# Row maxima taken by segments with a later look, and the row's own share added on VectorE

## The chip, the core and the metric

The kernel runs on one core of one Trainium2 chip, in one launch. The time is the device time of an execution in microseconds (us). The core has five engines that the text calls PE (TensorE, matrix products), DVE (VectorE), ACT (ScalarE), POOL (GpSimd) and SP (SyncE, which here only issues transfers). Each engine takes its instructions in the order in which the built program has them, and waits at an instruction until what it needs is there. Transfers between the device memory and the on-chip memory are issued by SP, by ACT and, where rows are picked by a list of indices, by POOL. An instruction of the kernel is named by its line, L623 say, and by the tile it writes and the tiles it reads, `tops<-ar`.

## The reference

Four graph layers follow each other on the same 2708 nodes with 512 features each. Each normalises x, applies relu, and adds its result to x. `adj` is a 2708 by 2708 matrix, almost all zeros, with entries of 0.05 to 5.42 where it is not zero, more of them at low node numbers.

```python
# layer 0
head = (adj > 0).astype(float)
head = head / maximum(sqrt(sum(head * head, -1, keepdims=True)), 1e-12)
inc = adj + head
x = x + (inc @ h) / sum(inc, -1, keepdims=True)
# layer 1: attention with the mask  -1e16 * (1 - maximum(adj, eye))
atts = atts - 1e16 * (1.0 - adj_with_diag)
x = x + softmax(atts) @ values @ Wo
# layer 2: two graph convolutions and a projection
# layer 3: (adj != 0) @ (h @ W + b) / column counts
```

In layer 1 the term 1e16 * adj is so large that each row's softmax picks one node: the column of the largest entry of `maximum(adj, eye)`. So layer 1 needs, for each row, the largest entry, its column, and the second largest entry (the kernel has a general path for the case that the two are too close, which these data do not take).

## The kernel before, in words

The rows are cut into 22 tiles m of 128 rows (`NT` = 22; the last has 20). The first stage, `with tc.tile_pool(name="l0_slab", ...)` up to L920, does layer 0, the search for the row maxima of layer 1, and the lists of nonzero columns that all later stages use. It takes the first 460 us. The instructions are ordered by a scheduler that plans with its own estimates of durations; the order on each engine is then fixed in the built program.

What is done for a row tile is spread over several functions:

- `stats_to(m)` runs ahead of the products: it loads the tile's rows of `adj` (a slab of 128 by 2708, `load_slab`, L563), counts signs and sums on ACT (`row_norm`, `row_sum`), and then calls `attended`. The tiles of `LATE` (0 to 5) are loaded again at the end of the stage, and `attended` is called for them there (L890 to L895).
- `attended(m)` (L617) sets the diagonal of the slab to at least 1 (L622) and searches the 2708 columns: `max` gives the eight largest entries of each row (L623), `max_index` their columns (L624). Only the first two values and the first column are used: `flags` compares the two values (L281), and `idx` (L914) is the list by which layer 1 fetches rows.
- `search(m)` finds the nonzero columns of a group from running counts (`max_index`, L461) and writes the indices `idx_g` and `idx_a`.
- `gathers_to(m)` issues on POOL, per chunk of 128 listed columns, one gather of entries of `adj` (`ac`, L635, 64 KB) and one of rows of the normalised x (`h`, L654, 256 KB). The row buffers are the tiles h6 to h21, so a gather has to wait until PE is done with what the buffer held. `CHUNKS` has 8 to 5 chunks per tile for the tiles 3 to 20.
- `incidence(m)` makes the weights: `inc` for the first (dense) column tiles and `incl` for the listed ones (L698, L706 on DVE). For the tiles 6 to 20 (`alone`), the diagonal entry is treated apart: ACT makes `own`, the row's own normalised x times its weight (L727), and the product of `ident` and `own` is one more pair in the sum (L728).
- The main loop (L854) multiplies the pairs on PE into `acc` (L866), scales by 1 over the degree and adds x on DVE (`xt`, L879), normalises, and one or two tiles later `after` makes the projection (`yacc`, L176) and stores `y`.

For the tiles 1 and 2 the entries are gathered at the end of the stage (L903) and stored to `listed` by POOL itself (L645). The next stage begins with `fetch` (L1166): a gather on POOL of rows of `y` by `idx` (L1172), which needs `idx` and every store of `y`.

DVE waits for ACT, PE and loads, and PE waits for DVE's `inc`; POOL waits for `idx_a` and `idx_g` from DVE, for the row buffers from PE and for the chunk buffers `ac` (three of them) from the stores to `listed`.

Of the kernel before, what the change touches and what calls it, by code (L numbers as in the profile page):

```python
# [9 lines left out]
FP = mybir.dt.float32  # L10
# [3 lines left out]
U32 = mybir.dt.uint32  # L14
U8 = mybir.dt.uint8
I32 = mybir.dt.int32
AF = mybir.ActivationFunctionType
ALU = mybir.AluOpType
AX = mybir.AxisListType
# [3 lines left out]
P = 128  # L23
LN_EPS = 1e-5
NORM_EPS = 1e-12
MASK_SCALE = 1e16
# [18 lines left out]
def kernel(  # L45
# [27 lines left out]
    nc = tc.nc  # L73

    N, D = x.shape
    H, _, DK = wk_d.shape
    NT = (N + P - 1) // P
    NFULL = N // P
# [4 lines left out]
    UNIT = 4  # L83
# [81 lines left out]
    nc.gpsimd.memset(ones_b, 1.0)  # L165


    adj_units = bass.AP(adj_t.tensor, 0, [[UNIT, N * N // UNIT], [1, UNIT]])

    def span(t):  # L170
# [73 lines left out]
    with tc.tile_pool(name="l0_slab", bufs=2) as slabs, tc.tile_pool(  # L244
        name="l0_h", bufs=1
# [14 lines left out]

        idx_a = hp.tile([P, NT, NCH], U32, name="idx_a")

        tops = hp.tile([P, NT, 8], FP, name="tops")
        at_top = hp.tile([P, NT, 8], U32, name="at_top")
        cnts, sums_sgn, ends, caps = (
            hp.tile([P, NT], FP, name=name) for name in ("cnts", "sums_sgn", "ends", "caps")
        )
# [5 lines left out]
        if TAIL:  # L273
            nc.gpsimd.memset(tops[:, NFULL, :], 0.0)
            nc.gpsimd.memset(tops[:, NFULL, 0:1], 2.0)
            nc.gpsimd.memset(at_top[:, NFULL, :], 0)

        def flags():

            score = wp.tile([P, NT, 2], FP, name="score", bufs=1)  # L280
            nc.vector.tensor_scalar(  # L281
                score, tops[:, :, 0:2], 1.0, MASK_SCALE, op0=ALU.subtract, op1=ALU.mult
            )
            nc.vector.tensor_tensor(bad[:, :NT], score[:, :, 1], score[:, :, 0], ALU.is_ge)
            nc.vector.tensor_tensor(
                bad[:, BAD_NEG : BAD_NEG + NT], sums_sgn, cnts, ALU.not_equal
            )
            nc.vector.tensor_tensor(bad[:, BAD_MANY : BAD_MANY + NT], ends, caps, ALU.is_gt)
# [17 lines left out]
        nc.gpsimd.iota(place_i, pattern=[[P, NCH]], base=1, channel_multiplier=1)  # L306
        places = hp.tile([P, NCH], FP, name="places")
        nc.vector.tensor_copy(places, place_i)

        pending, pending_c = [], []  # L310

# [253 lines left out]
        def count_signs(m, last):  # L565

            sgn = slabs.tile([P, N], BF, name="sgn", bufs=GROUP)
            behind(sgn[:1, :1], last)
            nc.scalar.activation(sgn, slab[m], AF.Sign, accum_out=sums_sgn[:, m : m + 1])
            nc.scalar.activation(sgn, sgn, AF.Relu, accum_out=cnts[:, m : m + 1])  # L570
# [46 lines left out]
        def attended(m):  # L617

            n = rows(m)
            cols = slice(m * P, m * P + n)  # L620
            ar = slab.pop(m)
            nc.vector.tensor_max(ar[:n, cols], ar[:n, cols], ident[:n, :n])  # L622
            nc.vector.max(tops[:n, m, :], ar[:n])  # L623
            nc.vector.max_index(at_top[:n, m, :], tops[:n, m, :], ar[:n])  # L624

        gathers, gather_slot = {}, [0]

# [60 lines left out]
        def incidence(m):  # L688
# [31 lines left out]
            if alone(m):  # L720
                c = diag_c[:, m : m + 1]
                by = wp.tile([P, 3], FP, name="by")
                nc.scalar.activation(by[:, 2:3], c, AF.Sign)
                nc.scalar.activation(by[:, 2:3], by[:, 2:3], AF.Identity, scale=rn, bias=c)
                nc.scalar.activation(by[:, :2], kept[:, :, m], AF.Copy, scale=by[:, 2:3])
                own = wp.tile([P, D], FP, name="own", bufs=1)
                nc.scalar.activation(own, xs[m], AF.Relu, scale=by[:, 0:1], bias=by[:, 1:2])  # L727
                pairs.append((ident, own))  # L728
            if m >= LEAD:
                ac, gs = gathers.pop(m)  # L730
                pending.append(lambda: nc.sync.dma_start(out=listed[m], in_=ac))
# [30 lines left out]
        def stats_to(m):  # L762


            while normed[0] <= order_n.index(m):
                t = order_n[normed[0]]
                do_next()
                load_slab(t)
                if normed[0] + 1 < NT:
                    load_slab(order_n[normed[0] + 1])  # L770
                row_norm(t)
                row_sum(t)
                if t == 0 or t % GROUP == GROUP - 1 or t >= NT - 2:
                    last_block = count(masks)
                    if t not in ZERO:
                        if dense_of(t):
                            rank_blocks(list(masks), last_block)
                        else:
                            flush_counts()
                            todo.append(partial(rank_rows, list(masks)))  # L780
                        todo.extend(partial(search, k) for k in masks)
                        do_next(0)
                    masks.clear()
                if t in LATE:
                    slab.pop(t)
                else:
                    attended(t)
                normed[0] += 1
# [65 lines left out]
        for m in range(NT):  # L854
# [37 lines left out]
                load_slab(LATE[step])  # L892
            if 0 < step <= len(LATE):
                count_signs(LATE[step - 1], xt[:1, :1])
                attended(LATE[step - 1])  # L895
            if m + 8 == NT + 1:
                todo.append(partial(rank_rows, list(range(1, LEAD))))
                todo.extend(partial(search, k) for k in range(1, LEAD))
# [12 lines left out]
                )  # L911
                wr = load_w(wset, w3_d, "wr")
        flush()
        nc.vector.tensor_copy(idx, at_top[:, :, 0])  # L914
        degrees()
        after(NT - 2, None)
        after(NT - 1, hns.pop(NT - 1))
# [1035 lines left out]
```

## Time and profile before

| what | value |
|---|---|
| time, median of 14 runs | 1352.41 us (1347.33 to 1361.07) |
| the profiled execution | 1352.61 us, span 1350.2 us |
| PE busy | 1199.0 us (89%) |
| DVE busy | 924.1 us (68%) |
| ACT busy | 694.3 us (51%) |
| POOL busy | 676.4 us (50%) |
| SBUF and HBM transfers | 349.92 MB, mean 259 GB/s |
| L623 and L624, 22 instructions each | 65.3 us each, mean 2970 and 2968 ns |
| gathers of entries `ac` on POOL (L635), 130 | 136.3 us, mean 1049 ns |
| gathers of rows `h` on POOL (L654), 111 | 115.8 us, mean 1044 ns |

The shares are of the whole span, over stages with different limits; the first stage is about a third of it. A row of a timeline gives the start and the duration in us, the engine, the line, the operation, out<-in, the shapes, and in brackets how long the engine had been idle and what ended that ("issue": nothing that the profile shows). A row of groups gives the count, then busy us and mean ns of one, then the idle time just before them. A row of waits gives who waited for whom, the us in total, the times, and the longest.

### The profile page before, as it was taken

What the parts mean: (1) busy time and instruction counts of PE and PEld (TensorE: products, weight loads), DVE (VectorE), ACT (ScalarE), POOL (GpSimd) and SP (SyncE); (2) the same over time, 40 slices, a digit from 0 to 9 for tenths busy, and PEclk for the clock granted to TensorE, in tenths of its full rate; (3) what the DMA queues carried; (4) which work ended last, traced back from release to release, by engine and by line L of the source; (5) the groups of instructions that cost most, each with busy time, mean ns of one, the idle gap of its engine ahead of it and who ended that gap; (6) DMA issues with size and microseconds to landing.
All of it is one profiled execution on the core that took longest, in us unless ns stands there. A gap on an engine that the chain in (4) does not pass through costs nothing.

```text
span 1350.2 us, 15148 instructions
## 1 busy us (share of the span) xinstructions
PE 1199.0 (89%) x4223; PEld 714.9 (53%) x4223; DVE 924.1 (68%) x1859; ACT 694.3 (51%) x1098; POOL 676.4 (50%) x703
## 2 busy tenths in 40 slices
PE   4988989998869389989999989899999999978897
PEld 2333444444423166646665656466666766656665
DVE  3777989998999589643444456256777677666676
ACT  5886377687365456432232334145555554555463
POOL 2237467777883511055554542354444444167763
PEclk9998999999889689999999999899999999988999
DMA  9988989999895697378877886866665656488885
GB/s 344 340 303 280 324 306 326 366 328 342 288 349 206 201 308 256 105 241 259 270 243 262 287 268 214 260 214 206 196 200 191 208 185 208 151 310 295 287 283 157
DMA packets 179341, 349.92 MB, mean 259 GB/s; under 512 B 22794, under 2 KB 85524, under 8 KB 175516
## 3 DMA queue, kind: packets, MB, share of 16 engines
q1 hardware_dynamic: 131648, 201.72, 44.0%
q0 software_dynamic: 46032, 145.05, 33.0%
q10 hardware_dynamic: 1568, 2.10, 0.4%
q8 instruction: 35, 0.57, 0.2%
q14 instruction: 58, 0.48, 0.1%
HBM read 285.97 MB, written 62.82 MB: 258 GB/s over the span
## 4 chain that ended last, share of the span: by engine, by line
PE 51%; DMA 21%; DVE 15%; issue 6%; POOL 3%; ACT 3%; SPq 1%; DVEq 0%; ACTq 0%; POOLq 0%
PE aggs L1110 14%; PE main L1010 8%; PE agg L1106 6%; PE mixed L1010 4%; PE acc L866 4%; PE yacc L176 3%; PE aggs L1106 3%; PE pt L983 2%; DVE found L461 2%; POOL ac L635 2%; DMA wb<-hid 2%; DMA nz<-nz 2%; DVE tops L623 2%; DMA h<-h0d,idx_g 1%; DMA ac<-g1d 1%
## 5 line engine op out<-in xcount | busy, mean ns | idle before, releaser
L1047 POOL DMA_INDIRECT gg<-g2d,idx_g x130 | 143.3, 1102 | 194.6 <-PE aggs L1110 138.7
L1110 PE MATMUL aggs<-gg,ac 128*128 128x512 f32 (+1 forms) x520 | 231.5, 593 | 2.9 <-DMA gg<-g1d,idx_g 2.1
L1047 POOL DMA_INDIRECT gg<-g1d,idx_g x130 | 131.3, 1010 | 155.3 <-PE aggs L1110 85.2
L635 POOL DMA_INDIRECT ac<-in_adj_t_dram,idx_a x130 | 136.3, 1049 | 69.6 <-issue 31.8
L866 PE MATMUL acc<-h,inc 128*128 128x512 f32 (+1 forms) x276 | 134.6, 631 | 27.7 <-DVE inc L706 22.5
L1110 PEld LDWEIGHTS aggs<-gg,ac 128*128 128x128 f32 (+1 forms) x520 | 96.9, 188 | 113.7 <-issue 99.3
L654 POOL DMA_INDIRECT h<-h0d,idx_g x111 | 115.8, 1044 | 47.0 <-issue 19.8
L866 PE MATMUL acc<-h,incl 128*128 128x512 f32 (+1 forms) x222 | 103.7, 607 | 0.0
L866 PEld LDWEIGHTS acc<-h,inc 128*128 128x128 f32 (+1 forms) x276 | 52.2, 201 | 86.4 <-issue 51.4
L176 PE MATMUL yacc<-wvo,hT 128*128 128x512 f32 (+1 forms) x176 | 83.8, 615 | 1.4 <-ACT hT L211 1.4
L1075 DVE SCALAR_TENSOR_TENSOR ac<-ac,diag_c,bias 128x512 f32<-128x512 f32 x30 | 22.6, 752 | 88.1 <-DMA ac<-g1d 53.8
L1047 POOL DMA_INDIRECT gg<-hidr,idx_g x62 | 66.5, 1072 | 27.8 <-issue 13.9
L1106 PE MATMUL agg<-glo,a_lo 128*128 128x512 f32 x180 | 73.5, 408 | 4.6 <-ACT glo L225 4.6
L1106 PE MATMUL agg<-ghi,a_hi 128*128 128x512 f32 x180 | 77.3, 430 | 0.0
L1106 PE MATMUL aggs<-gs,a_s 128*128 128x512 f32 x180 | 73.5, 408 | 1.3 <-DVE gs L222 1.3
L990 DVE SCALAR_TENSOR_TENSOR v_lo<-pt,v_hi 128x512 fp32r<-128x512 f32 (+1 forms) x88 | 56.8, 656 | 16.1 <-ACT v_hi L989 15.8
L866 PEld LDWEIGHTS acc<-h,incl 128*128 128x128 f32 (+1 forms) x222 | 41.1, 191 | 48.4 <-issue 43.6
L1139 DVE SCALAR_TENSOR_TENSOR u<-aggs,u 128x512 f32<-128x512 f32 x42 | 28.8, 687 | 55.0 <-PE aggs L1110 54.8
L623 DVE MAX8 tops<-ar 128x8 f32<-128x2708 f32 (+1 forms) x22 | 65.3, 2970 | 0.0
L624 DVE FIND_INDEX8 at_top<-tops,ar 128x8 uint32<-128x2708 f32 (+1 forms) x22 | 65.3, 2968 | 0.0
L583 ACT ACTIVATE sgn<-ar 128x2708 bf16<-128x2708 f32 (+1 forms) x22 | 54.1, 2458 | 17.1 <-DMA ar<-in_adj_dram 17.1
L989 ACT ACTIVATE v_hi<-pt 128x512 fp32r<-128x512 f32 (+1 forms) x88 | 48.1, 575 | 24.9 <-PE pt L983 24.8
(355 smaller groups left out, 2758.8 us busy)
## 6 DMA issues: line engine op xcount, KB each, us to landing
ar<-in_adj_dram SPq DMA_DIRECT2D x27, 1354.0 KB
raw<-in_adj_t_dram SPq DMA_DIRECT2D x92, 192.0 KB
slot<-x SPq DMA_DIRECT2D x41, 256.0 KB
at<-in_adj_t_dram SPq DMA_DIRECT2D x26, 256.0 KB
h<-in_x_dram SPq DMA_DIRECT2D x21, 256.0 KB
h0d<-h POOLq DMA_DIRECT2D x21, 256.0 KB, 7.4
xt<-in_x_dram SPq DMA_DIRECT2D x21, 256.0 KB
x<-xt SPq DMA_DIRECT2D x21, 256.0 KB
```

Of the source, the lines that this page charges most:

```text
L176: nc.tensor.matmul(acc[:n], hT[:, c, :n], w[:, c, :], start=(c == 0), stop=(c == NCD - 1))
L583: nc.scalar.activation(sgn[:n], ar[:n], AF.Sign, accum_out=sum_sgn[:n])
L623: nc.vector.max(tops[:n, m, :], ar[:n])
L624: nc.vector.max_index(at_top[:n, m, :], tops[:n, m, :], ar[:n])
L635: nc.gpsimd.indirect_dma_start(out=ac[:, c, :n], out_offset=None, in_=adj_units, element_offset=dense_of(m) * P * N + m * P, in_offset=bas ...
L654: nc.gpsimd.indirect_dma_start(out=g, out_offset=None, in_=h0d[:, :], in_offset=bass.IndirectOffsetOnAxis(ap=index_g(m)[:, c : c + 1], axi ...
L866: product = nc.tensor.matmul(acc[:n], a, g, start=(i == 0), stop=(i == len(pairs) - 1))
L990: nc.vector.scalar_tensor_tensor(lo[d], pt[d], 0.0, hi[d].bitcast(FP), op0=ALU.max, op1=ALU.subtract)
L1010: nc.tensor.matmul(acc[:n], a[:, c, :n], b[:, c, :], start=first and c == 0, stop=last and c == NCD - 1,)
L1047: nc.gpsimd.indirect_dma_start(out=gs[c], out_offset=None, in_=gd[:, :], in_offset=bass.IndirectOffsetOnAxis(ap=index_g(m)[:, c : c + 1], ...
L1106: turn(nc.tensor.matmul(acc[:n], a[:k, i, :n], b[:k], start=st, stop=sp))
L1110: nc.tensor.matmul(mixed[:n], a, g, start=(c == 0 and not dense_of(m)), stop=(c == len(chunks) - 1),)
```

## The change

Two parts of the first stage are written differently.

The maxima: for a full tile `attended` no longer searches the whole row twice. It takes the maximum of each segment of 128 columns (the last segment is the 20 columns left over), then the largest and second largest of these 22 maxima (`peaks`) and the segment of the largest. From its start it computes, for each row, the place of that segment in `adj` (in units of four entries). A new function `look`, called at the places where `attended` is called, gathers that segment again from the device memory on POOL (`win`, 128 by 128, one indirect transfer), and, for the segment gathered three calls earlier, puts the diagonal in, finds the two largest values and the column, and completes `tops` and `at_top`. The second largest of the row is the larger of the second peak and the second value in the segment. The short last tile is searched as before. At the end of the stage the looks that are left are done before `idx` is copied.

The own share: `own` is also multiplied by the row's 1 over degree, and added to x on DVE ahead of the sum, in place of the pair (`ident`, `own`) on PE.

```diff
+    row_units = bass.AP(adj.tensor, 0, [[UNIT, N * N // UNIT], [1, UNIT]])
...
-        tops = hp.tile([P, NT, 8], FP, name="tops")
-        at_top = hp.tile([P, NT, 8], U32, name="at_top")
+        tops = hp.tile([P, NT, 2], FP, name="tops")
+        at_top = hp.tile([P, NT], U32, name="at_top")
...
+        row_i = hp.tile([P, 1], I32, name="row_i")
+        nc.gpsimd.iota(row_i, pattern=[[0, 1]], base=0, channel_multiplier=N // UNIT)
+        row_unit = hp.tile([P, 1], FP, name="row_unit")
+        nc.vector.tensor_copy(row_unit, row_i)
...
             nc.vector.tensor_max(ar[:n, cols], ar[:n, cols], ident[:n, :n])
-            nc.vector.max(tops[:n, m, :], ar[:n])
-            nc.vector.max_index(at_top[:n, m, :], tops[:n, m, :], ar[:n])
+            if n < P:
...
+                return
+            segs = wp.tile([P, NT], FP, name="segs", bufs=1)
+            near_w = NFULL * P
+            nc.vector.tensor_reduce(
+                segs[:, :NFULL],
+                ar[:, :near_w].rearrange("p (s w) -> p s w", w=P),
+                AX.X,
+                ALU.max,
+            )
+            nc.vector.tensor_reduce(segs[:, NFULL:], ar[:, near_w:], AX.X, ALU.max)
+            peaks = wp.tile([P, 8], FP, name="peaks", bufs=5)
+            nc.vector.max(peaks, segs)
+            best = wp.tile([P, 8], U32, name="best", bufs=1)
+            nc.vector.max_index(best, peaks, segs)
+            begin = wp.tile([P, 1], FP, name="begin", bufs=5)
+            nc.vector.tensor_scalar(
+                begin, best[:, 0:1], float(P // UNIT), float((N - P) // UNIT), op0=ALU.mult, op1=ALU.min
+            )
+            place = wp.tile([P, 1], U32, name="place", bufs=2)
+            nc.vector.tensor_scalar(place, begin, row_unit[:, 0:1], None, op0=ALU.add)
+            segments.append((m, begin, place, peaks))
+
+        segments, windows = [], []
+
+        def look():
+
+            if windows and (len(windows) == 3 or not segments):
+                m, begin, win, peaks = windows.pop(0)
+                own = wp.tile([P, 1], FP, name="own_seg")
+                nc.vector.tensor_scalar(
+                    own, begin, float(m * P // UNIT), None, op0=ALU.is_equal
+                )
+                nc.vector.scalar_tensor_tensor(
+                    win, ident, own[:, 0:1], win, op0=ALU.mult, op1=ALU.max
+                )
+                high = wp.tile([P, 8], FP, name="high", bufs=1)
+                nc.vector.max(high, win)
+                where = wp.tile([P, 8], U32, name="where", bufs=1)
+                nc.vector.max_index(where, high, win)
+                nc.vector.tensor_max(tops[:, m, :], peaks[:, 0:2], high[:, 0:2])
+                nc.vector.scalar_tensor_tensor(
+                    at_top[:, m : m + 1],
+                    begin,
+                    float(UNIT),
+                    where[:, 0:1],
+                    op0=ALU.mult,
+                    op1=ALU.add,
+                )
+            if segments:
+                m, begin, place, peaks = segments.pop(0)
+                win = wp.tile([P, P], FP, name="win", bufs=3)
+                nc.gpsimd.indirect_dma_start(
+                    out=win,
+                    out_offset=None,
+                    in_=row_units,
+                    element_offset=m * P * N,
+                    in_offset=bass.IndirectOffsetOnAxis(ap=place[:, 0:1], axis=0),
+                )
+                windows.append((m, begin, win, peaks))
...
                 nc.scalar.activation(by[:, 2:3], by[:, 2:3], AF.Identity, scale=rn, bias=c)
+                nc.scalar.activation(by[:, 2:3], by[:, 2:3], AF.Copy, scale=row[m][1])
                 nc.scalar.activation(by[:, :2], kept[:, :, m], AF.Copy, scale=by[:, 2:3])
                 own = wp.tile([P, D], FP, name="own", bufs=1)
                 nc.scalar.activation(own, xs[m], AF.Relu, scale=by[:, 0:1], bias=by[:, 1:2])
-                pairs.append((ident, own))
+                nc.vector.tensor_add(xs[m], xs[m], own)
...
                     masks.clear()
+                look()
                 if t in LATE:
                     slab.pop(t)
                 else:
                     attended(t)
...
                 count_signs(LATE[step - 1], xt[:1, :1])
+                look()
                 attended(LATE[step - 1])
+            elif normed[0] == NT:
+                look()
...
         flush()
-        nc.vector.tensor_copy(idx, at_top[:, :, 0])
+        while segments or windows:
+            look()
+        nc.vector.tensor_copy(idx, at_top)
         degrees()
```

## The prediction

> **What bounds the kernel now.** The change touches only the first stage (0 to about 460 us), so I read the busy time by stretches of 25 us first, then POOL's waits, then the POOL and DVE timelines.
>
> Busy us (and instructions) of PE, PEld, DVE, ACT, POOL; then granted clock, DMA share, GB/s:
>
> ```profile
> 200.00:225.00 25.00, 24.48 (x90) 11.21 (x89) 23.55 (x51) 16.76 (x28) 19.20 (x20) 1.00 0.99 354
> 300.00:325.00 25.00, 24.18 (x96) 10.94 (x94) 23.03 (x51) 16.43 (x25) 18.57 (x20) 1.00 1.00 356
> 400.00:425.00 25.00, 24.11 (x65) 10.96 (x64) 25.00 (x36) 12.22 (x15) 11.16 (x13) 1.00 0.73 279
> ```
>
> ```profile
> POOL ac L635 <- issue: 24.5, 80, 0.4
> POOL h L654 <- issue: 19.8, 65, 0.3
> POOL h L654 <- PE acc L866: 19.3, 20, 10.9
> ```
>
> The 19.2 us hide a full queue: 20 gathers of 0.94 us with 0.30 us between fill 25 us. From 175 to 405 us POOL issues one gather per 1.25 us without a break. DVE is nearly full too, and after 340 the chain of waits is mostly DVE.
>
> ```profile
> 115.97 0.95 POOL L654 DMA_INDIRECT h<-h0d,idx_g  x1 [0.30 <-DMA ac<-in_adj_t_dram,idx_a]
> 145.70 0.94 POOL L654 DMA_INDIRECT h<-h0d,idx_g  x1 [10.95 <-PE acc L866]
> 173.56 0.94 POOL L635 DMA_INDIRECT ac<-in_adj_t_dram,idx_a  x1 [4.92 <-DMA lst<-ac]
> 418.37 0.94 POOL L635 DMA_INDIRECT ac<-in_adj_t_dram,idx_a  x1 [10.49 <-DVE inc L706]
> 431.06 0.59 POOL L645 DMA_DIRECT2D lst<-ac  x1 [2.94 <-DMA ac<-in_adj_t_dram,idx_a]
> 440.91 0.97 POOL L635 DMA_INDIRECT ac<-in_adj_t_dram,idx_a  x1 [0.30 <-issue]
> 460.73 1.11 POOL L1172 DMA_INDIRECT slot<-y,idx  x1 [5.23 <-DMA bias<-in_L_gnn_b_dram]
> ```
>
> POOL's only long pauses are those bracketed waits. The row at 460.73 opens the next stage: it needs `idx` and the last `y` store.
>
> ```profile
> 118.00 0.22 DVE L612 SCALAR_TENSOR_TENSOR deg<-cnts,rn,rsum 128x1 f32<-128x1 f32 x1 [2.34 <-ACT ar L611]
> 137.66 0.74 DVE L879 SCALAR_TENSOR_TENSOR xt<-acc,deg,xt 128x512 f32<-128x512 f32 x1
> 439.88 0.29 DVE L622 TENSOR_TENSOR ar<-ar,ident 128x128 f32<-128x128 f32 x1 [1.82 <-ACT sgn L569]
> 446.25 0.15 DVE L281 TENSOR_SCALAR score<-tops 128x44 f32<-128x44 f32 x1
> 446.33 0.16 DVE L914 COPY idx<-at_top 128x22 uint32<-128x22 uint32 x1
> 462.69 0.22 DVE L1514 TENSOR_REDUCE some<-bad 128x1 f32<-128x67 f32 x1
> ```
>
> Prices (count | busy, mean ns | idle before); the last row's 5.1 is us from issue to landing:
>
> ```profile
> L623 DVE MAX8 tops<-ar 128x8 f32<-128x2708 f32 x21 | 62.4, 2971 | 0.0
> L866 PE MATMUL acc<-own,ident 128*128 128x512 f32 x30 | 15.3, 592 | 0.0
> L706 DVE TENSOR_TENSOR inc<-inc,at 128x512 f32<-128x512 f32 x26 | 17.6, 682 | 0.1
> L595 DVE SCALAR_TENSOR_TENSOR dg<-ar,ident 128x128 f32<-128x128 f32 x15 | 4.1, 276 | 1.7 <-DMA ar<-in_adj_dram 1.7
> ac<-in_adj_t_dram,idx_a POOLq DMA_INDIRECT x130, 5.1
> ```
>
> **The change, part by part.**
>
> *DVE, maxima.* Removed per full tile (21): MAX8 and FIND_INDEX8 over 2708, starts 6.0 us apart to the next work. Added: a reduction over 2688 in 21 segments (by MAX8's slope 2.95 us), one over 20, MAX8 and FIND over 22, `begin`, `place`: small operations start 0.08 to 0.1 us apart (446.25, 446.33), so 0.65 together, 3.6 in all. The later look adds two more searches over 128 and a 128x128 product at 0.28 each (row L595), and four small ones: 1.2. Balance 4.8 - 6.0 = -1.2, times 21 = -25 us. Bounds: with every small operation at its full 0.15 to 0.2 us, -0.6 x 21 = -13; if each segment also paid 0.15 us (67 elements cost 0.22, so 0.15 is fixed), 21 x 21 x 0.15 = 66 more. I take -25: MAX8 is the nearest long row.
>
> The Trainium skill, "VectorE: DVE Perf Modes", section "The TRN2 errata", speaks against this part: a fixed 150 cycles or so per instruction, paid by each of many small ones. By that the twelve small operations would cost an estimated 2 us per tile and the gain would be nearly gone. The rows show the duration but also starts 0.08 us apart.
>
> *Own share.* 15 products leave PE (15.3 us busy). DVE gets 15 adds at 0.68 = +10 us; ACT 15 scalings at 0.3 = +4.5, hidden, ACT being busy 12 to 17 of 25 (4.5 if that cover is gone). PE's relief I cost at 0: where POOL or DVE ends a tile, PE only waits longer; if PE paced the whole stage it would be -15. The setup's iota and the short last tile's two copies are under 0.5. DVE's balance is -15 us, from -3 to +50. The slab comes free one FIND earlier; SP's slab loads waited 21.4 us for it in total, none of it on the chain: 0.
>
> *POOL.* 21 window gathers at 1.25 = +26 us, 15 of them before POOL reaches 330 us, in a queue that has no gap. The 1.4 MB they move are about 4 us of transfer at 350 GB/s, between gathers that POOL paces: 0 (at most 4). SP issues the same DMAs, partly in another order; 0, at most one landing of 5.
>
> *New waits.* In this part the numbered windows are the new gathers in POOL's order. DVE now waits for landed windows, POOL for `place`. In the built program's order, behind such a wait stand the `inc` and `xt` steps that PE needs, and behind POOL's the row gathers. I walk the built order along the old timeline.
>
> 1. Early. Window 1 stands behind the 22 gathers `ac` of tiles 3 to 5: issued 114.7, landed 120; DVE is there at 115 (118 with the old wait for ACT). Window 2 stands behind eight row gathers: 114.7 + 9 x 1.25 = 126.0, landed 131. DVE waits there from 121, then needs 8 us (reduction, two `inc`, a scan's head) to `place` of window 3 at 139, which POOL (there at 137) waits for; it lands at 145. Behind that wait stand the last `inc` of tile 2, so its `xt` slips from 137.7 to 154, and the row gather that waited until 145.7 for PE to free a buffer goes at 157. Window 4 follows two gathers later and waits for a `place` that DVE reaches at 161. POOL is then 14 us late; of this the pauses at 166 (2.2) and 173 (4.9) swallow 7.
>
> 2. Middle. POOL keeps +7, +2.6 for two row gathers now ordered behind those of `ac`, and 1.25 per window: +11 at the eighth window (old place 234, landing 251, DVE's use 238), +14 at the eleventh (281, landing 301, DVE's use 283). So DVE, lightened by some 5 us between, is held to +13 and then +18. From 325 on DVE alone paces: five maxima (-2.4 each for the first half), one look (+1.2), six adds (+0.7): about +10 at 425. POOL, +23 after 18 windows, still lands rows before PE needs them (by the trace's landings rows of tiles 15 to 21 came 6 to 20 us ahead of their products).
>
> 3. Tail. POOL reaches tile 1's late `ac` at 408 + 23 + 1.25 = 432 instead of 418.4. Old distances from there: list store +12.7, two `ac` +16, end +18.4. Window 19 goes there, lands at 456; another list store and nine `ac` (9 x 1.25) follow, then window 20: issued 466.5, landed 472. On DVE window 20's use stands ahead of the last big reduction and of tile 20's `rstd` (old place 440). From 472: reduction 3 us, `rstd`, `hn`, transposes, `yacc` of tiles 20 and 21, store. The old distance from `rstd` (440.1) to the fetch (460.7) is 20.6, of which 3.0 went to the MAX8 between; 475 + 17.6 gives 492.6. The last window (`place` 478, landed 484, `idx` 485) is earlier. 492.6 - 460.7 = +32 us. The later stages are the same instructions and move with it.
>
> The Trainium skill, "DMA: Bandwidth & Descriptors", section "Anatomy of one DMA", has 2.0 us fixed plus bytes / 436 GB/s for a DMA from POOL: 2.2 us for a window where the rows say 5.1. By the page each wait would end 3 us earlier and the sum would be an estimated +27. The measured 5.1 decides.
>
> **Sum.** The profiled run took 1352.61 us (span 1350.2), the median is 1352.41. 1352.6 + 32 = 1384.6, less the 0.2 to the median: 1384.
>
> **Rivals.**
> - *DVE and PE win (faster).* If windows land before DVE asks, DVE's -15 would show where DVE paces (about half of the stage): 1352 - 8 = 1344. It decides at window 2: POOL would have to issue it before 112, ahead of the eight row gathers. POOL's full queue speaks against it. 4%. No visible change: 2%.
> - *Only the tail.* POOL's lateness is absorbed by 425 because PE, lighter by 15 us, lets DVE catch up. Then the late `ac` start at 418.4, window 20 goes at 453.4, lands at 458.5, against 440: +18, 1370. For it: POOL's 10.49 pause at 418. Against: POOL has no other slack. 25%.
> - *POOL's length alone.* The order holds, the tail wait hides behind other work: 15 x 1.25 = +19, 1371. 8%.
> - *Dear reduction.* 0.15 us per segment, 66 us of DVE, half of it in stretches where DVE would wait anyway: 1384 + 30 = 1414. 6%.
> - *Forecast*, both body and tail: 1384, 55%.
>
> **How the numbers follow.** Cases within 0.3% (4 us, about what this kernel's runs can tell apart) hold 2%, faster 4%, slower 94%. The range starts under the two cases at 1370 (5 us for a shorter landing) and ends at 1398, half-way to the dear reduction. Left out are that case, the two fast ones and the outer parts of the others, some 2 in 10.
>
> **What would show it.** Right: DVE waiting for DMA `win` for some 10 us before 150 and over 10 us near 460; POOL waiting for DVE `place` twice before 165; the first `slot<-y` near 492; TENSOR_REDUCE at 2.9 to 3.0 us; POOL pitch still 1.25. Wrong: no DVE wait at `win`, a window landing in 2 us, or POOL with gaps after 175.

## The result and the profile after

The changed kernel takes 1389.66 us (median of 10 runs, 1379.83 to 1396.53), beside 1352.95 us of the kernel before (47 runs): a ratio of 1.027, 95% interval 1.0243 to 1.0298. It is slower. Ratios here and below are those of the record, over fast runs alone, and can differ by some 0.2% from the quotient of two medians. The profiled execution took 1388.85 us with a span of 1387.1 us, 36.9 us more than the span before.

The lines below answer to those shown of the kernel before. First POOL's timeline of the changed kernel (start and duration in us; in brackets the idle time before and what ended it). L687 is the window gather, L705 the entries `ac`, L724 the rows `h`, L1249 the first gather of the next stage.

```profile
115.98 0.95 POOL L687 DMA_INDIRECT win<-in_adj_dram,place  x1 [0.31 <-issue]
127.23 0.94 POOL L687 DMA_INDIRECT win<-in_adj_dram,place  x1 [0.30 <-DMA h<-h0d,idx_g]
139.09 1.33 POOL L687 DMA_INDIRECT win<-in_adj_dram,place  x1 [0.30 <-issue]
158.60 0.95 POOL L724 DMA_INDIRECT h<-h0d,idx_g  x1 [18.18 <-PE acc L938]
161.10 0.94 POOL L687 DMA_INDIRECT win<-in_adj_dram,place  x1 [0.30 <-issue]
...
437.72 0.94 POOL L705 DMA_INDIRECT ac<-in_adj_t_dram,idx_a  x1 [2.60 <-DMA lst<-ac]
...
470.69 0.95 POOL L687 DMA_INDIRECT win<-in_adj_dram,place  x1 [0.30 <-DMA ac<-in_adj_t_dram,idx_a]
...
495.53 1.30 POOL L1249 DMA_INDIRECT slot<-y,idx  x1 [15.39 <-ACT wb L226]
```

The same stretches on DVE. L668 is the first instruction that needs a landed window, L951 the `xt` step.

```profile
119.40 0.35 DVE L668 SCALAR_TENSOR_TENSOR win<-ident,own_seg,win 128x128 f32<-128x128 f32 x1 [6.62 <-DMA win<-in_adj_dram,place]
130.77 0.35 DVE L668 SCALAR_TENSOR_TENSOR win<-ident,own_seg,win 128x128 f32<-128x128 f32 x1 [10.09 <-DMA win<-in_adj_dram,place]
137.65 0.20 DVE L655 TENSOR_SCALAR place<-begin,row_unit 128x1 uint32<-128x1 f32 x1
145.29 0.35 DVE L668 SCALAR_TENSOR_TENSOR win<-ident,own_seg,win 128x128 f32<-128x128 f32 x1 [5.62 <-DMA win<-in_adj_dram,place]
153.15 0.74 DVE L951 SCALAR_TENSOR_TENSOR xt<-acc,deg,xt 128x512 f32<-128x512 f32 x1
...
249.53 0.35 DVE L668 SCALAR_TENSOR_TENSOR win<-ident,own_seg,win 128x128 f32<-128x128 f32 x1 [7.68 <-DMA win<-in_adj_dram,place]
250.13 0.74 DVE L951 SCALAR_TENSOR_TENSOR xt<-acc,deg,xt 128x512 f32<-128x512 f32 x1
...
458.40 0.35 DVE L668 SCALAR_TENSOR_TENSOR win<-ident,own_seg,win 128x128 f32<-128x128 f32 x1 [3.77 <-DMA win<-in_adj_dram,place]
...
473.30 0.35 DVE L668 SCALAR_TENSOR_TENSOR win<-ident,own_seg,win 128x128 f32<-128x128 f32 x1 [13.40 <-DMA win<-in_adj_dram,place]
473.56 2.95 DVE L639 TENSOR_REDUCE segs<-ar 128x21 f32<-128x2688 f32 x1
476.43 0.15 DVE L200 RECIPROCAL rstd<-rstd 128x1 f32<-128x1 f32 x1
```

DVE stands idle for window 1, 2 and 3, then at window 8, for 3.8 us at window 19 and for 13.4 us at window 20 (and for 1.2 and 2.6 us at windows 11 and 21). Behind the first three waits tile 2's `xt` slips from 137.66 to 153.15. POOL waits 18.2 us for PE until 158.6, where it had waited 10.95 until 145.70. Behind the wait at 473.30 stand the last big reduction and tile 20's `rstd`, and so the last `y` and the gather at 495.53, which was at 460.73.

The sums of these waits, and the new groups of instructions (count | busy us, mean ns of one | idle us before):

```profile
DVE win L668 <- DMA win<-in_adj_dram,place: 50.9, 8, 13.4
POOL h L724 <- PE acc L938: 24.4, 19, 18.2
```

```profile
L639 DVE TENSOR_REDUCE segs<-ar 128x21 f32<-128x2688 f32 x21 | 61.7, 2940 | 0.0
L687 POOL DMA_INDIRECT win<-in_adj_dram,place x21 | 20.3, 965 | 11.4 <-DVE rstd L200 5.6 <-issue 3.1 <-DVE segs L645 0.6
L799 DVE TENSOR_TENSOR xt<-xt,own 128x512 f32<-128x512 f32 x15 | 10.1, 676 | 1.8 <-ACT own L798 1.8
L668 DVE SCALAR_TENSOR_TENSOR win<-ident,own_seg,win 128x128 f32<-128x128 f32 x21 | 7.2, 340 | 50.9 <-DMA win<-in_adj_dram,place 50.9
```

DVE's work did become shorter: its busy time over the whole span fell from 924.1 to 902.7 us. The 50.9 us in which it now waits for windows are new. By stretches of 25 us (busy us and instructions of PE, PEld, DVE, ACT, POOL; granted clock, DMA share, GB/s):

```profile
300.00:325.00 25.00, 25.00 (x70) 11.73 (x69) 25.00 (x74) 19.43 (x30) 19.30 (x19) 1.00 0.89 291
325.00:350.00 25.00, 23.30 (x94) 10.99 (x93) 19.70 (x52) 14.60 (x27) 18.32 (x20) 1.00 1.00 371
350.00:375.00 25.00, 15.61 (x35) 7.41 (x35) 21.04 (x54) 9.63 (x19) 16.11 (x17) 0.73 0.85 263
375.00:400.00 25.00, 25.00 (x68) 11.68 (x67) 21.59 (x41) 12.74 (x22) 17.88 (x16) 1.00 0.78 271
400.00:425.00 25.00, 16.38 (x37) 7.45 (x36) 22.98 (x44) 15.71 (x19) 20.92 (x12) 0.80 0.95 327
```

From 325 to 425 DVE is busy 85.3 us (19.70 + 21.04 + 21.59 + 22.98); before it was 96.4. It no longer fills this stretch, and the rows gain little by it: over these 100 us their lateness falls from 20.9 us (tile 12) to 17.1 (tile 18).

Where the 36.9 us are, by the starts of three instructions in the two traces: tile 20's `xt` moved from 435.2 to 452.5 (+17.3, the body); from there to the first `slot<-y` it took 25.5 us before and 43.0 now (+17.5, the tail); the rest of the span grew by 2.1. The tail's two waits for windows, 3.8 and 13.4 us, sum to 17.2.

The body is less simple. The `xt` of tile 2 is 15.5 us later than before, but that of tile 3 only 6.9 and that of tile 4 only 2.6. Tile 5 is 10.1 us late, tile 7 21.4, and from there to tile 20 it is between 15.7 and 24.0. So on the rows most of the lateness of the first three waits is made up by tile 4. On POOL it is not: its gathers, counted within their kind, are 14 us later than before near 150, still 10 to 12 from 230 to 250, and 20 near 340. So the later windows are issued late too. After tile 4 there are two kinds of waits. Between the `xt` of tiles 4 and 5 DVE waits for no window, but 4.3 us for loaded ranks and 1.7 for ACT. Between those of tiles 6 and 7 it waits 7.7 us for window 8 and 4.3 for ACT:

```profile
225.58 0.81 ACT L798 ACTIVATE own<-xt,by 128x512 f32<-128x512 f32 x1 [9.52 <-DMA xt<-in_x_dram]
227.59 0.16 DVE L200 RECIPROCAL rstd<-rstd 128x1 f32<-128x1 f32 x1 [4.25 <-ACT rstd L199]
```

ACT had stood 9.5 us for a loaded tile of x, and its part of `rstd` came behind that. Such waits of ACT ahead of `own` add up to 53.0 us (12 times) here and 14.3 us (twice) before. What they add to the body, and why the loads came late, is not shown.

### The profile page after: what moved, and what is told of

It reads as the page before. It is cut to its first block, busy times and chain, and to the rows that moved or that the text cites. A ratio compares the mean times of both kernels' runs of the same rounds, so it can differ in the third digit from the quotient of the medians.

```text
span 1387.1 us, 15369 instructions
## 1 busy us (share of the span) xinstructions
PE 1200.4 (87%) x4193; PEld 718.0 (52%) x4193; DVE 902.7 (65%) x2108; ACT 695.0 (50%) x1113; POOL 694.2 (50%) x725
## 4 chain that ended last, share of the span: by engine, by line
PE 42%; DMA 11%; DVE 4%; issue 3%; ACT 2%; POOL 2%; SPq 0%; DVEq 0%; ACTq 0%; POOLq 0%
PE aggs L1187 13%; PE main L1087 8%; PE agg L1183 5%; PE mixed L1087 4%; PE aggs L1183 3%; DMA gg<-hidr,idx_g 2%; PE pt L1060 2%; PE agg L1397 1%; PE aggs L1397 1%; DMA ac<-g2d 1%; DMA g2d<-go 1%; PE agg L1087 1%; PE aggs L1201 1%; POOL gg L1124 1%; DMA wa<-hidr,idx_g 1%
## 5 line engine op out<-in xcount | busy, mean ns | idle before, releaser
L938 PE MATMUL acc<-h,inc 128*128 128x512 f32 (+1 forms) x276 | 146.3, 675 | 35.2 <-DVE inc L776 29.7
L705 POOL DMA_INDIRECT ac<-in_adj_t_dram,idx_a x130 | 130.9, 1007 | 61.3 <-issue 34.7
L724 POOL DMA_INDIRECT h<-h0d,idx_g x111 | 118.3, 1066 | 54.3 <-PE acc L938 24.4
L938 PEld LDWEIGHTS acc<-h,inc 128*128 128x128 f32 (+1 forms) x276 | 55.6, 214 | 97.3 <-issue 55.1
L938 PE MATMUL acc<-h,incl 128*128 128x512 f32 (+1 forms) x222 | 99.2, 594 | 0.0
L1045 ACT ACTIVATE go<-main 128x512 f32<-128x512 f32 (+1 forms) x33 | 19.6, 593 | 86.5 <-PE main L1087 85.3
L1087 PE MATMUL main<-wb,v_hi 128*128 128x512 f32 (+1 forms) x176 | 57.0, 445 | 6.0 <-ACT v_hi L1066 4.9
L639 DVE TENSOR_REDUCE segs<-ar 128x21 f32<-128x2688 f32 x21 | 61.7, 2940 | 0.0
```

The lines of the kernel that those rows point to most:

```text
L639: nc.vector.tensor_reduce(segs[:, :NFULL], ar[:, :near_w].rearrange("p (s w) -> p s w", w=P), AX.X, ALU.max,)
L705: nc.gpsimd.indirect_dma_start(out=ac[:, c, :n], out_offset=None, in_=adj_units, element_offset=dense_of(m) * P * N + m * P, in_offset=bas ...
L724: nc.gpsimd.indirect_dma_start(out=g, out_offset=None, in_=h0d[:, :], in_offset=bass.IndirectOffsetOnAxis(ap=index_g(m)[:, c : c + 1], axi ...
L938: product = nc.tensor.matmul(acc[:n], a, g, start=(i == 0), stop=(i == len(pairs) - 1))
L1087: nc.tensor.matmul(acc[:n], a[:, c, :n], b[:, c, :], start=first and c == 0, stop=last and c == NCD - 1,)
```

## The experiments

The experiments ran on three chips on which the kernel before takes about 1430 us and not 1353 (more on that at the end), so only ratios to the kernel before on the same chip are compared. The parts alone, the run without transfers and the unread gathers share one chip; the full searches share the second; the held looks, the three cures and the changed kernel itself the third. That a ratio carries over from one of them to another is assumed. Each variant is also scheduled anew, so that the order of other instructions shifts a little too, and each has one profile alone. The changed kernel itself, without an edit, was run on the third again, so that the experiments have a reference:

> The changed kernel once more, beside the experiments, because the chip of the experiments runs the kernel before in 1431.7 us and not in 1353. If the loss is the same on this chip: ratio 1.024 to 1.030. If PE, which pauses more often on this chip, paces so much of the stage that DVE's and POOL's waits are partly covered: 1.015 to 1.022.

Measured: 1460.36 against 1429.29 us, ratio 1.0236 (1.0205 to 1.0267). That is just below the first of the two bands, and its interval reaches into it: the loss is there on this chip too, perhaps a little smaller. DVE's waits for windows add up to 31.7 us here. The one before the end is the same, with the same two instructions behind it (DVE's timeline):

```profile
524.81 0.35 DVE L668 SCALAR_TENSOR_TENSOR win<-ident,own_seg,win 128x128 f32<-128x128 f32 x1 [13.44 <-DMA win<-in_adj_dram,place]
525.08 2.95 DVE L639 TENSOR_REDUCE segs<-ar 128x21 f32<-128x2688 f32 x1
527.94 0.15 DVE L200 RECIPROCAL rstd<-rstd 128x1 f32<-128x1 f32 x1
```

**The two parts, each alone.** The maxima without the own share:

```diff
-                nc.scalar.activation(by[:, 2:3], by[:, 2:3], AF.Copy, scale=row[m][1])
...
-                nc.vector.tensor_add(xs[m], xs[m], own)
+                pairs.append((ident, own))
```

> Only the maxima part of the change: segments and later looks, with the row's own share still a product of ident and own on PE. Theory (the windows' waits make the loss, the own share is worth little): 1382 to 1390 us, because in the changed kernel DVE's waits at win are in the same places. Rival 1 (the loss comes in part from the 15 adds on DVE, +10 us of DVE): 1372 to 1380. Rival 2 (PE's 15.3 us of relief had softened the loss): above 1393.

Measured: ratio 1.0189 (1.0123 to 1.0256), which on the 1352.4 us of the first runs is 1378 us. The point lies in the band of the first rival; the interval (1369 to 1387) reaches into the theory's band too, so the run does not decide between them.

The own share without the maxima (the kernel before with these lines):

```diff
+                nc.scalar.activation(by[:, 2:3], by[:, 2:3], AF.Copy, scale=row[m][1])
...
-                pairs.append((ident, own))
+                nc.vector.tensor_add(xs[m], xs[m], own)
```

> Only the own share: scaled on ACT and added to x on DVE, the maxima as before. Theory: the 10 us more on DVE and the 15.3 us less on PE nearly cancel; after 340 us, where DVE paces, six adds of 0.68 make +4: 1350 to 1358 us, most likely 1354. Rival 1 (DVE full in the whole stage): +10, 1362. Rival 2 (PE paces, its relief shows): 1340 to 1346.

Measured: ratio 1.006 (1.0026 to 1.0094), 8.1 us on 1352.4. The theory had +2 and at most +6; the value lies nearer to the rival by which DVE is full in the whole stage (+10), and the interval (3.5 to 12.7) reaches both. So the own share alone is not neutral: ten more microseconds on DVE and 15.3 fewer on PE cost about eight together; the run does not part the two. The product of the two ratios is 1.025, close to what the whole change has, so the maxima are about three quarters of the loss if the parts do not affect each other (a run below suggests that they do).

**The work without the transfers.**

```diff
+        still = hp.tile([P, P], FP, name="still")
+        nc.gpsimd.memset(still, 0.0)
...
-                win = wp.tile([P, P], FP, name="win", bufs=3)
-                nc.gpsimd.indirect_dma_start(out=win, ...)
-                windows.append((m, begin, win, peaks))
+                windows.append((m, begin, still, peaks))
```

> The changed kernel with the window gathers left out: the looks read a tile that was zeroed at the start, so the column inside the segment and the second value of the row are not searched in the row's entries. DVE's instructions and ACT's and PE's stay. Theory (the loss is all in the waits for windows and POOL's longer queue; DVE's work by itself became 15 us shorter): 1340 to 1350, most likely 1344 as the fast case of the forecast had it. Rival (the new DVE instructions themselves cost, in small operations or in the order they force): above 1356.

Measured: ratio 0.9953 (0.9924 to 0.9982), 1346 us on the scale of the first runs. DVE's new instructions are cheaper than the old ones and the gain shows, some 6 us of it (2 to 10), as long as nothing has to be fetched. The rival (the new instructions cost by themselves) is out.

**POOL's length without the waits.** The kernel before with 21 gathers that nothing reads:

```diff
+                win = wp.tile([P, P], FP, name="win", bufs=3)
+                nc.gpsimd.indirect_dma_start(
+                    out=win, out_offset=None, in_=row_units, element_offset=m * P * N,
+                    in_offset=bass.IndirectOffsetOnAxis(ap=row_unit[:, 0:1], axis=0),
+                )
```

> The kernel before with 21 window gathers more on POOL, at the same places in the program, of a fixed segment (the first of each row) that nothing reads and that waits for no place. It isolates what 21 x 1.25 = 26 us in POOL's queue cost without any wait of DVE for a window or of POOL for a place. Theory (the waits make the loss): the pauses of POOL at 146 to 173 and at 418 swallow most of it, and 1352 to 1360 comes out, most likely 1356. Rival (POOL's length alone): 15 x 1.25 = +19 or more, 1371 to 1378.

Measured: ratio 1.0009 (0.9971 to 1.0047). This reads like the theory, but the profile says that the run did not test it. The gathers of that one line on POOL (least, median and largest duration in ns, then the first and the last start in us):

```profile
L641 POOL DMA_INDIRECT win<-in_adj_dram,row_unit x21: 942/947/1037, 22.4 to 67.8; - x21
```

All 21 gathers ran between 22 and 68 us, where POOL has little to do (in the kernel before it is busy for 9.8 of these 46 us). They wait for nothing that is made later, so the scheduler put them at the start, whatever their place in the program. The run tells nothing of POOL's length in the body.

**Full searches at the two ends.** In the next runs some tiles take the old search, so their windows are gone. The late tiles:

```diff
-            if n < P:
+            if n < P or m in (0, 1, 2, 3, 4, 5):
                 high = wp.tile([P, 8], FP, name="high", bufs=1)
```

> The changed kernel, but the six tiles 0 to 5 that are searched at the end of the stage are searched in full as before (MAX8 and FIND_INDEX8 over 2708), so there are 15 windows instead of 21 and none after 360 us. In the changed kernel's trace the last xt but one was 17 us late and the first slot<-y 35 us. Theory (two places: a late body and a tail wait): the tail's half goes, the full searches give back some 4 us of DVE, so 20 to 23 us above before: ratio 1.012 to 1.019. Rival (the body's lateness decides, and another wait takes the place of the one for window 20): ratio 1.024 or more. Rival (the tail is all of it): 1.006 or less.

Measured: ratio 1.016 (1.0119 to 1.0202), in the theory's band. In its profile the stretch from tile 20's `xt` to the first `slot<-y` is 29.0 us (521.0 to 550.1), where the changed kernel on the third chip has 41.7 (505.5 to 547.2).

The early tiles (the same line with `m in (6, 7, 8, 9)`):

> The changed kernel, but the first four tiles that are searched (6 to 9) are searched in full as before, so the windows 1 to 4, at which DVE waited 22 us before 150, are gone and POOL's queue is four gathers shorter there; the tail keeps its windows. Theory (the early waits make POOL and the rows late, which is carried to the end): about 9 us of the lateness of the body goes, the tail's wait stays: ratio 1.018 to 1.022. Rival (the early lateness is swallowed before 425 in any case): no change against the changed kernel, 1.025 to 1.030.

Measured: ratio 1.0133 (1.0099 to 1.0167), a larger gain than the theory had: 0.0103 of 1430, some 15 us, where 9 were expected. The wait before the end is still there (13.5 us at window 16, the last but one of these 17), and 42 us pass from tile 20's `xt` to the first `slot<-y`. The early windows are thus worth some 15 us at the end and are not swallowed. The path is not tested by itself. In the first two traces the rows had made up most of this lateness by tile 4 and POOL had not, so POOL's queue is the likely one; the run also frees it of four gathers.

Both ends at once (`m in (0, 1, 2, 3, 4, 5, 6, 7, 8, 9)`), first with the own share on DVE, then as a product on PE:

> Both at once: full search for the tiles 0 to 9, segments and windows only for the eleven tiles 10 to 20, and the own share added on DVE as in the changed kernel. Theory (early and tail waits make most of the loss, and they add): about 12 us above before, ratio 1.006 to 1.012, of which 1.006 would be the own share alone. Rival (POOL's eleven longer steps and the waits in the middle are enough): 1.015 or more.

Measured: ratio 1.0025 (0.9991 to 1.0059), better than the theory's band of 1.006 to 1.012. If the two ends add, 1.0236 - 0.0076 - 0.0103 = 1.0057 is left, just inside the interval.

> The same with the own share as a product on PE, as before: eleven tiles with segments are all that is left of the change. Theory: the eleven windows land before they are asked for, DVE saves 11 x 1.2 = 13 us where it paces half of the time, POOL's 11 x 1.25 = 14 us lie where it has pauses: ratio 0.995 to 1.003. Rival (the middle windows wait too): 1.008 or more. Rival (the gain on DVE shows in full): 0.990.

Measured: ratio 1.0038 (1.0003 to 1.0073), just above the theory's band. Eleven tiles with segments gain nothing. Between these two runs the place of the own share makes no difference that can be told (the intervals overlap), where it cost 0.6% alone; why it costs in the one setting and not in the other stays open.

**The looks held back.** By the program, a window is looked into three calls after its gather was issued. In the built order of the changed kernel the use of windows 1 and 2 stands right after `place` of the second searched tile, and that of window 3 right after the third: the scheduler, which plans with its own durations, pulled the looks forward. This run forbids it with an ordering edge on DVE alone (no wait), with one window buffer more and `best` in the buffer of `where`:

```diff
-            best = wp.tile([P, 8], U32, name="best", bufs=1)
+            best = wp.tile([P, 8], U32, name="where", bufs=1)
...
-            nc.vector.tensor_scalar(place, begin, row_unit[:, 0:1], None, op0=ALU.add)
+            last_place[:] = [nc.vector.tensor_scalar(place, ..., op0=ALU.add).ins]
...
                 m, begin, win, peaks = windows.pop(0)
-                own = wp.tile([P, 1], FP, name="own_seg")
-                ...
+                with tc.issue_after(last_place[0]):
+                    own = wp.tile([P, 1], FP, name="own_seg")
+                    ...
-                win = wp.tile([P, P], FP, name="win", bufs=3)
+                win = wp.tile([P, P], FP, name="win", bufs=4)
```

> The changed kernel with the looks held back: in the built order the use of a window may not stand before place of the row tile that is attended last at that point of the program (with four window buffers in place of three). In the changed kernel's order windows 1 and 2 are used right after place of tile 2 and window 3 right after place 3, so one tile later and not three; here they are used after place 4, 5 and 6. Theory (DVE's waits at windows 1 to 3, 8 and 11 make the body late): these waits are gone, POOL's 26 us stay and lie mostly in its pauses, and the tail keeps its wait for the last windows: ratio 1.010 to 1.018. Rival (the body's lateness is POOL's length, not the waits): 1.025 or more.

Measured: ratio 1.0015 (0.998 to 1.0051). All 21 window gathers are in POOL's queue, at most seven places from where the changed kernel has them, the own share is on DVE, and DVE has the same instructions; the order differs, and with it 0.022 of the 0.0236 is gone. So the 26 us more in POOL's queue do not make the loss by themselves, which the run with the unread gathers had left open. They may still cost a part of the 0.006 between this ratio and the 0.9953 without transfers; no run parts them from the waits that remain. By the two profiles tile 20's `xt` comes 8.5 us earlier than in the changed kernel (497.1 for 505.5) and the tail is 12.0 us shorter (29.7 for 41.7); tile 18's `xt` is no earlier (478.9 for 477.8), so where in the body the gain is made is not shown. DVE's timeline of this kernel before the end, with POOL's first gather of the next stage:

```profile
504.51 0.15 DVE L200 RECIPROCAL rstd<-rstd 128x1 f32<-128x1 f32 x1
504.90 2.94 DVE L639 TENSOR_REDUCE segs<-ar 128x21 f32<-128x2688 f32 x1
508.47 0.14 DVE L200 RECIPROCAL rstd<-rstd 20x1 f32<-20x1 f32 x1
509.01 0.61 DVE L669 SCALAR_TENSOR_TENSOR win<-ident,own_seg,win 128x128 f32<-128x128 f32 x2
520.61 0.35 DVE L669 SCALAR_TENSOR_TENSOR win<-ident,own_seg,win 128x128 f32<-128x128 f32 x1 [10.33 <-DMA win<-in_adj_dram,place]
524.03 0.35 DVE L669 SCALAR_TENSOR_TENSOR win<-ident,own_seg,win 128x128 f32<-128x128 f32 x1 [2.00 <-DMA win<-in_adj_dram,place]
525.68 0.18 DVE L992 COPY idx<-at_top 128x22 uint32<-128x22 uint32 x1
526.79 1.35 POOL L1250 DMA_INDIRECT slot<-y,idx  x1 [4.29 <-ACT wb L216]
```

There is no early wait left (window 1, issued at 117, is used at 163). The wait for window 20 is still 10.3 us, but now the last reduction and both `rstd` stand ahead of it, and the first `slot<-y` comes at 526.79, 20.4 us earlier than in the changed kernel on the same chip. The theory had expected the tail's loss to stay (1.010 to 1.018). It had not seen that the same edge also moves the last looks behind the work that `y` needs. The wait is not free there either: `idx` stands behind it, and the first `slot<-y` follows `idx` by 1.1 us. It starts 9.8 us after the last `yo` (517.02, the last step of `y` on ACT), where in the first two profiles this takes 4.0 us (before) and 3.8 (after). So about 6 of the 10.3 us are still paid, an estimate from these distances. A wait of the same kind costs less where only `idx` is queued behind it than where `y` is.

**All three cures together:** looks held, late tiles searched in full, own share on PE.

> The looks held back as in the run before, the six late tiles searched in full, and the own share as a product on PE: 15 windows, none of which DVE should wait for. Theory: DVE's saving of 15 x 1.2 = 18 us against POOL's 15 x 1.25 = 19 us: ratio 0.995 (what the kernel without transfers had) to 1.002. Rival (windows wait wherever they are put): 1.008 or more.

Measured: ratio 1.005 (1.0022 to 1.0077), above the theory's band. DVE waits for windows 2.4 us in all, and still this is not faster than the run before it; why is open. No version of the change that fetches its windows beats the kernel before; the nearest is the one with the looks held, at 1.0015.

## Why the prediction was right, and where it was off

The forecast was 1384 us, with a range from about 1365 to 1398; measured 1389.66. The places of loss are the ones that were forecast, body and tail, and the tail's wait is as described. That the sum is only 6 us short is in part luck: the body came out 7 us longer than its term and the tail 4.5 us shorter.

*Early.* The times of the walk along the built order hold to within 2 us. Window 1: forecast 114.7, landed 120; measured 115.98, used 119.40. Window 2: 126.0 and 131; 127.23 and 130.77. Window 3: 139 and 145; 139.09 and 145.29. Tile 2's `xt` 154; 153.15. The row gather 157; 158.60. Window 4 161; 161.10. One reason in it is wrong: POOL was to wait for `place` at windows 3 and 4. It did not; `place` was there at 137.85 and 159.81, and both gathers went 0.30 us after the one ahead of them, so they stood in POOL's queue. On POOL the lateness lasts as the walk has it: 14 us near 150, 6.5 at 175, then 10 to 12 where the eighth window stands (forecast 14, 7 and 11). The rows make theirs up for a time: tile 4's `xt` is 2.6 us late.

*Middle.* Window 8 was put at 234 + 11 = 245, landed 251; measured 244.1 and 249.53. Window 11 at 295, landed 301; 293.5 and 299.8, but DVE waited there only 1.2 us, since it was late already. What failed is the step "from 325 on DVE alone paces ... about +10 at 425". Tile 18's `xt` came at 426.2 and not 409.2, +17. The rows entered this stretch 21 us late (tile 12) where the step starts from 18, and made up 4 us where it has 8. DVE was busy 11 us less between 325 and 425 and was idle in as much, in waits of 1 to 3.5 us each for ACT, for loads and for PE: a relieved DVE was no longer the only pace. The run without transfers agrees: of DVE's saving (forecast 15 us, measured 21.4 of busy time in the whole change) some 0.5% of the time is seen (0.2 to 0.8). A second thing was put at nearly nothing, the loads in another order ("0, at most one landing of 5"): ACT's waits for tiles of x grew from 14.3 to 53.0 us, and one of them held DVE for 4.3.

*Tail.* The late `ac` were put at 432; they started at 437.72: at the gather ahead of them POOL was 26 us late and not 23, and a window and a wait of 2.6 us for a store came between. Window 20 was put at 466.5 and landed at 472; measured 470.69, used 473.30. The two errors cancel in part: the issue was 4 us later, the landing took 2.6 us in place of 5.1. The first fetch was put at 492.6 and came at 495.53. The later stages, put at 0, added 2.1. So the terms were mis-sized as body 10 (measured 17.3) and tail 22 (measured 17.5).

*Signs.* DVE's waits at `win` (22.3 us before 150, where some 10 were named, and 13.4 near 470), the length of the reduction and POOL's 1.25 us per gather came as named. POOL's two waits for `place` before 165 did not; it waited so only at window 21, for 5.3 us. And one of the signs of being wrong was seen: POOL stood still after 175, for 6.2 us until 377.22, for a store to `listed`; its other waits up to 430 are under 1.3 us.

*Landing of a window.* The single price of 5.1 us was wrong on both sides. Where DVE waited, the time from the start of the issue to the use was 3.4, 3.5, 6.2, 5.5 and 6.3 us in the body (windows 1, 2, 3, 8, 11) and 2.5, 2.6 and 2.8 us in the tail (windows 19 to 21). The DMA engines were 36 to 51% busy in the few microseconds around the last three, 58 to 61% around windows 1 and 2, and 70 to 93% around windows 3, 8 and 11. By the fit in the Trainium skill, "DMA: Bandwidth & Descriptors", section "Anatomy of one DMA", a transfer of this size takes an estimated 2.2 us; the trace comes near that in the quiet tail alone.

*Maxima on DVE.* The reduction took 2940 ns (forecast 2.95 us); there is no price per segment, and the dear-reduction rival is out. DVE's balance was put at -15; its busy time fell by 21.4. The Trainium skill, "VectorE: DVE Perf Modes", section "The TRN2 errata", by whose fixed cost per instruction the gain would nearly have gone, does not agree with this: from 446.25 to 449.56 DVE starts 26 instructions, most of three looks among them, 0.13 us each, which makes about 1 us for a look of seven.

*Own share.* Its +10 us on DVE went into DVE's balance and PE's relief was put at 0, so the sum has no price for it. Alone it costs 0.6% (0.3 to 0.9). With the tiles 0 to 9 searched in full its place made no difference that can be told, so its price in the changed kernel is not settled.

*Rivals.* "Only the tail" falls, since tile 18's `xt` is 17 us late and the late `ac` start at 437.72 and not at 418.4. "POOL's length alone" (+19 us, a ratio of 1.014) falls by the held looks. "DVE and PE win" has its price confirmed (0.994 forecast, 0.9953 without transfers) and its condition corrected: the prediction said that POOL would have to issue window 2 before 112. The runs show a second way, that DVE asks later, by an ordering edge; it takes the early waits away but does not bring the gain (1.0015).

## What to carry to other kernels

A distance that the program gives ("looked into three tiles later") is not the distance in the built order, where a scheduler may pull the use forward to the moment at which it believes the data to be there. Read the use of every new transfer in the built order, and list what stands behind it on its engine: this decides the price of the wait, as the two ends of this stage show (13.4 us before `rstd`, paid in full; 10.3 us after it, an estimated 6). And before a busy engine is relieved, see how far the next limits are; here DVE ran into waits of 1 to 3.5 us for ACT, PE and loads. An experiment whose instruction depends on nothing must be looked up in its profile too, since it may have run somewhere else.

## What the runs showed of the hardware that was not expected

The kernel before took a median of 1429 to 1432 us on the three chips of the experiments, and 1353 where the first two profiles were taken. A profile of it, without an edit, was taken there to see why:

> The kernel before, for a profile on the chip of the experiments. Expected: ratio 1, and in the first stage pauses of PE of some 10 us inside runs of matrix products (20 us for 30 products that take 2.3 us otherwise), which the first profile does not have.

Its one profiled execution took 1421.2 us. The first `slot<-y` starts at 518.7 in place of 460.7, so 58 of the 69 us lie in the first stage. Between 100 and 400 PE is busy for 228.8 us there and 264.1 in the first profile, DVE 217.6 and 273.2, and the stage has five pauses of PE of 8 to 17 us (at 114, 234, 299, 359 and 439), where the first profile has two of 7 and 12; so the expectation that the first profile has none was too strong. Nor do the pauses lie inside the runs of products: each run of 30 takes 2.27 to 2.31 us in this profile. The pauses at 234, 299 and 359 come behind such a run: PE waits for DVE, DVE for ACT, and ACT 19.3, 9.7 and 12.0 us, to copy what the run has made, for something that the profile does not name. In the changed kernel on the same chip the run itself is slow, here one of 30 small matrix products (PE's timeline; L331):

```profile
177.40 1.79 PE L331 MATMUL list<-sgn,counts 128*32 128x512 bf16 x19
179.83 0.38 PE L331 MATMUL list<-sgn,counts 128*32 128x512 bf16 x1 [0.64 <-issue]
181.26 0.38 PE L331 MATMUL list<-sgn,counts 128*32 128x512 bf16 x1 [1.05 <-issue]
183.35 0.18 PE L331 MATMUL list<-sgn,counts 128*32 128x37 bf16 x1 [1.71 <-issue]
185.45 0.19 PE L331 MATMUL list<-sgn,counts 128*32 128x37 bf16 x1 [1.92 <-issue]
188.25 0.19 PE L331 MATMUL list<-sgn,counts 128*32 128x37 bf16 x1 [2.60 <-issue]
190.36 0.37 PE L331 MATMUL list<-sgn,counts 128*32 128x256 bf16 x1 [1.92 <-issue]
```

and the granted clock (third number from the end) in the same microseconds:

```profile
177.00:180.00 3.00, 2.36 (x23) 1.01 (x21) 0.84 (x8) 0.81 (x1) 2.39 (x3) 1.00 1.05 391
180.00:184.00 4.00, 0.77 (x3) 0.18 (x2) 0.00 (x0) 0.00 (x0) 2.72 (x4) 1.00 0.81 290
184.00:188.00 4.00, 0.19 (x1) 0.20 (x2) 0.00 (x0) 0.00 (x0) 3.08 (x4) 0.61 0.47 119
```

The first 19 products take 1.8 us, the other eleven the rest; the starts of the first six of these lie 1.43, 2.09, 2.10, 2.80 and 2.11 us apart, close to multiples of 0.70 us. Such a run of 30 takes 2.3 us in the changed kernel's first profile, 18.7 here. The eleven wait for nothing that the profile shows, and the granted clock is still 1.00 when the slow pitch begins; it falls after the pause has begun, so a lower clock is not what starts it. DVE and ACT stand idle meanwhile. What holds PE back on these chips, whether the pauses of the kernel before have the same cause, and whether it explains the whole difference of 77 us, is open. Both kernels are slower there, and the ratio of the two came out nearly the same (1.0236 and 1.027).
